# Two-layer graph network, 128 graphs: W3's product of the first quad by two levels of Winograd's form, a list of steps of its own for six periods, and another order within a period

## The chip, the cores and the metric

The kernel runs on one core of a Trainium2 chip. The metric is the device time of one launch in microseconds, lower is better. Everything is fp32.

## The reference

There are B = 128 graphs with N = 128 nodes and F = 512 features: x is [128, 128, 512], adj [128, 128, 128]. Two layers follow one another, each a residual step with a layer norm:

```python
deg = jnp.sum(adj, axis=-1, keepdims=True)                      # layer 0
agg = jnp.einsum('bij,bjf->bif', adj, x) / jnp.maximum(deg, 1e-6)
x = layernorm(x + relu(jnp.concatenate([x, agg], 2) @ W.T))     # W: 512 x 1024
h = relu(adj @ (x @ W1) + b1)                                   # layer 1
h = relu(adj @ (h @ W2) + b2)
x = layernorm(x + adj @ (h @ W3) + b3)                          # W1, W2, W3: 512 x 512
```

## The kernel before, in words

**Quads and products.** The graphs are taken in 32 quads of four (`NG = 32`, `G = 4`). Of a quad, the 512 x 512 matrix of its nodes and features is multiplied with each of the weights: twice for layer 0 (the halves of W that meet x and agg), then W1, W2, W3. Each is done in Winograd's form of Strassen's method. One level means seven products of blocks of 256, each of four matmuls 128x256 (`product`, L596), reached through `rows_a`/`rows_b` or `wino_a`/`wino_b`. Two levels mean that each of the seven is again split in seven, 49 matmuls in all, of 128x128 (`inner_product`, L614), reached through `single_a`/`single_b`. These need inner forms of both factors (`inner_sums`): those of the data are made for each quad by POOL, or by DVE, and lie in the small `ti` buffers; those of W2 and W3 are made once, on DVE, and lie in the large buffer `big` in place of the layer-0 weights `wb` and `wa`. From quad 2 on, the two layer-0 products are done together by two levels (`joint_a`/`joint_b`, matmuls 128x256 of L614), with forms of the weights that were written to DRAM once (`forms`) and stream back through the buffers `ring` and parts of `big`. Quads 0 and 1 do layer 0 by one level. In the kernel before, quad 0 does all of layer 1 by one level (`two(q)` is q >= 1), quads 1 to 30 do W2 and W3 by two levels and W1 by one, and quad 31 has forms of its own at the end.

**Stages.** The work of a quad is cut into stages, each a Python generator:

- X loads x transposed and makes its sums; D loads adj (`ar`), sums it to degrees on DVE (`deg`), sends their reciprocals to DRAM in another order (`dd<-deg`, elements of 4 bytes) and back to all partitions (`ah<-dd`); AT loads adj transposed (`at`).
- L0 to L3 are layer 0's products. A0 and A1 load x itself (`s<-in_x_dram`), copy the half of the product with x into a PSUM bank on ACT (L885), add adj times the other half on PE (L889), take relu and add x on DVE (L896), and do the layer norm (statistics on DVE, L828 and L829; the normalization on ACT, L859).
- G0 to G3 multiply with adj on PE (L914) and copy the result to SBUF; Ha and Hb are W1's product (L596); Sa and Sb W2's; H2 multiplies with adj (L1002) and applies bias and relu on ACT (L1013); Ta and Tb are W3's product; Z0 and Z1 multiply with adj (L1109), add the residual, do the second layer norm and store.

Between two groups of matmuls of a product the banks are moved: ACT copies a bank to SBUF (`copied`, L576) or to another bank that the next matmuls add to (`seeded`, L582), DVE adds a bank and a buffer (all of `add` for DVE has line L325, for POOL L327). All DMAs have line L318; SP issues nearly all of them, and waits in its queue for the buffer of each.

**The order of the work.** It is written before the kernel is emitted. `ORDER` is a list of stages with lags: "L3-4" in period t is the next part of stage L3 of quad t − 4. A period goes through the list once; a stage that comes up before its conditions hold (`AFTER`) is put off until they do. Steps create operations, and the class `Plan` then lists each engine's operations in a fixed order, by due times worked back from PE's and by costs that it assumes for each kind of operation. It has constants: `AHEAD` (how far down PE's list it may look), `HELP` (how late a POOL operation must be for DVE to take it), `REST`, and `LEADS` (how far ahead of their due time some operations may be listed); `SIZES` gives the numbers of buffers `s`, `v`, `ti` and `ring`. At run time each engine does its operations strictly in that order. `AFTER` says of W3's product only that it follows H2. Work that is done once hangs on finished stages (`posts`): layer 0's forms are made after L3 of quad 0, W2's inner forms after L2 and L3 of quad 1 and Sb of quad 0, W3's after L2 and L3 of quad 1 and Tb of quad 0.

Of the kernel before, what the change touches and what calls it, by code (L numbers as in the profile page):

```python
# [35 lines left out]
class Plan:  # L36
# [5 lines left out]


    LAG = 0.15
    AHEAD, HELP, HOLD, SEEN, REST, SPARE = 32, 16.0, 5.0, 8, 15.0, 1
    DMA_US, DMA_RATE = 2.0, 0.22e6

    def __init__(self, pools):
# [175 lines left out]


BANKS = 8
SIZES = 8, 3, 7, 6
LEADS = 6.9, 7.0, 29.0, 448.5
AFTER = {
    "X": "L2-1+1 L3-1+1", "D": "A0-1 A1-1 D-1", "AT": "Z0-2 Z1-2", "L0": "X D AT A1-1 A0-1 Z0-2 Z1-2", "L1": "L0", "L2": "L1", "L3": "L1 L2<2",  # L230
    "A0": "L2 L3", "A1": "L2 L3", "G0": "A0 Hb-1", "G1": "A0 Hb-1", "G2": "A1 Hb-1", "G3": "G0 G1 G2 A1",
    "Ha": "G3 Tb-1!", "Hb": "Ha", "Sa": "Hb Z0-1! Z1-1!", "Sb": "Sa", "H2": "Sb", "Ta": "H2", "Tb": "Ta", "Z0": "Ta Tb!", "Z1": "Tb",
}
ORDER = """
    L3-4 L0-4 Ta-6 H2-5 L3-4 Tb-5 Sa-5 L1-4 L1-4 Hb-5 D Tb-6 L2-4 L3-4 G0-4 Z0-6 Sb-4 D L2-4 L2-4 Tb-5 L0-3 L0-3 L1-4
    Ta-5 Ha-4 A1-4 L1-4 L3-3 Tb-5 Sb-4 X-3 Tb-5 A0-4 Ha-4 L2-4 L3-3 Ha-4 Ha-4 H2-5 H2-5 H2-5 Hb-4 L0-3 Tb-5 Tb-5 H2-5
    L3-4 L2-4 L2-4 Sb-4 L1-3 L2-4 L0-3 Z1-6 Sb-4 L3-3 Ta-5 Sb-4 Ta-5 G3-4 AT-3 A0-3 Ta-5 G2-4 Z0-5 L3-3 Z0-5 G2-4 Sa-4
    Ha-3 Ta-5 Tb-5 A1-4 Ha-3 Sb-4 G1-4 Sa-4 Sb-4 L0-3 G3-4 Sb-4 L1-3 Sa-4 Sa-4 Sa-4 Sa-4 Z1-5 A0-4 L1-3 G1-4 Z1-6 L2-3
    Hb-4 G0-4 AT-3 Ta-5 X-2 L1-3 Ta-5 L0-3 A1-3 Sa-4 L0-3
"""  # L240


# [1 line left out]
def gnn_resnorm_kernel(  # L244
# [16 lines left out]
    NG, F = x.shape[0], 512  # L261
# [7 lines left out]

    NS, NV, NI, NR = SIZES  # L270
    EARLY = 2
# [35 lines left out]
    def pinned(ins):  # L307
        return tc.keep_in_program_order(ins)
# [4 lines left out]
    def scalar(n, emit, reads, writes, columns=0, lead=None):  # L313
        plan.op("ACT", 0.165 + 0.00083 * n + 0.1 * columns, emit, reads, writes, lead=lead)

    def dma(dst, src, reads, writes, size, queue="SP", lead=None):
        eng = nc.sync if queue == "SP" else nc.scalar
        plan.op(queue, 0.06, lambda: pinned(eng.dma_start(dst(), src())), reads, writes, size=size, lead=lead)  # L318

    def const(v):  # L320
        return lambda: v

    def add(eng, n, dst, a, b, reads, writes, op=OP.add, shared=False, lead=None):

        on_vector = lambda: pinned(nc.vector.tensor_tensor(dst(), a(), b(), op=op))  # L325
        if eng == "POOL":
            on_gpsimd = lambda: pinned(nc.gpsimd.tensor_tensor(dst(), a(), b(), op=op))  # L327
            plan.op("POOL", 0.03 + 0.00243 * n, on_gpsimd, reads, writes, True, other=(0.06 + 0.00123 * n, on_vector), lead=lead)
        else:
            vector(n, on_vector, reads, writes, shared)  # L330
# [90 lines left out]
    class Streamed:  # L421

        def parts(self, ps, i):
# [3 lines left out]
                lambda: RING_T[s.index][:, 0:n], const(FORMS[i - 1][:, ps[0] : ps[-1] + 1].rearrange("p k s n -> p k (s n)")),  # L427
                ["ring free"] + [("form", w, i, p) for w in range(2) for p in ps], [s], n * P * H * 4, lead=LEADS[3],
            )
            return [lambda j=j: RING_T[s.index][:, j] for j in range(n)], [s]  # L430

    class Data:
# [18 lines left out]
        def inner_sums(self):  # L451
            for ps in PAIRS:
# [13 lines left out]
                for dst, a, b, reads, writes, op in (  # L466
# [4 lines left out]
                ):  # L471
                    add("POOL", n * P, dst, a, b, reads, writes, op, lead=LEADS[2] if dst is first else None)

# [38 lines left out]
    def data(q, name):  # L512
        if (q, name) not in TS:
            i = int(name != "g1")
            alone = q == NG - 1 and name != "g1"
            TS[q, name] = Data("xT", XT_T) if alone else Data(f"T{i}", T_T[i])
        return TS[q, name]

    def row(q, name):
        i = int(name != "y" and q < NG - 1)  # L520
        return Rows(f"row{i}", ROW_T[i])
# [46 lines left out]
    def quarters(p, n):  # L568
        return bank_ap(p).rearrange("p a (b n) -> p (a b) n", n=P)[:, 0:n]
# [50 lines left out]
    def v_part(v, n, g, c):  # L620
        return lambda: V_T[v.index][:, 0:n, g, c]
# [56 lines left out]
    def last_part(a, b, ps, joint, v, kv, sinks):  # L678
# [18 lines left out]

        scalar(n * P, lambda: pinned(nc.scalar.copy(quarters(pz, n), v_part(v, n, 1, 1)())), kv, [pz], lead=LEADS[0])
        add("POOL", n * P, v_part(v, n, 0, 1), v_part(v, n, 0, 1), v_part(v, n, 1, 1), kv, [(v, "d")], OP.subtract)
# [180 lines left out]
    def seg_agg(q, m):  # L880
        y, u = l0(q)
        for g in (2 * m, 2 * m + 1):
            p, r = Slot("bank", seeded=True), Slot("s", spare=3)
            dma(lambda r=r: S_T[r.index].rearrange("p a b -> p (a b)"), const(x[q][:, g]), (), [r], P * F * 4, lead=LEADS[1])
            scalar(512, lambda g=g, p=p: pinned(nc.scalar.copy(bank_ap(p), u.graph(g))), u.keys((g,)), [p], lead=LEADS[0])  # L885
            plan.op(
# [78 lines left out]
    def two(q):  # L965
        return q >= 1
# [25 lines left out]
    def seg_h2(q):  # L992
        d, s = data(q, "h2"), row(q, "s2")
        a, ka = at(q)
        for o in (2, 3, 0, 1):
            p = Slot("bank")
            h, c = o // 2, o % 2

            def emit(o=o, p=p):
                for g in range(G):  # L1000
                    r = pinned(
                        nc.tensor.matmul(  # L1002
                            bank_ap(p)[:, g // 2, (g % 2) * P : (g % 2 + 1) * P],
                            s.chunk(g, o), a[:, g, :], start=g == 0, stop=True, skip_group_check=True,
                        )
                    )
                return r

            plan.op("PE", 0.888, emit, ka + s.keys(cs=(o,)), [p])
            scalar(  # L1010
                512,
                lambda o=o, p=p, h=h, c=c: pinned(
                    nc.scalar.activation(  # L1013
                        d.t[:, 4 * h : 4 * h + 2, c], bank_ap(p).rearrange("p m (g n) -> p m g n", g=2), AF.Relu,
                        bias=B2_T[:, o : o + 1],
                    )
                ),
                [p, "b2"], d.keys((4 * h, 4 * h + 1), (c,)), columns=1,
            )
            yield  # L1020
        d.sums(at_end=q == NG - 1)
        if two(q) and q < NG - 1:
            d.inner_sums()

    def columns_a(key, a, b, t):
# [59 lines left out]
    def seg_s3_a(q):  # L1085
        if q == NG - 1:
            W3.restore()
            yield from rows_at_end_a(("s3", q), data(q, "h2"), W3, row(q, "s3"))
            return
        yield from (single_a if two(q) else rows_a)(("s3", q), data(q, "h2"), W3, row(q, "s3"))  # L1090

    def seg_s3_b(q):
        if q == NG - 1:
            yield from rows_at_end_b(("s3", q), data(q, "h2"), W3, row(q, "s3"))
            return
        yield from (single_b if two(q) else rows_b)(("s3", q), data(q, "h2"), W3, row(q, "s3"))

    def seg_last(q, m):
        s, u = row(q, "s3"), u_of(q)
# [2 lines left out]
        for j, o in enumerate(os):  # L1102
            g = 2 * m + j
            p = Slot("bank", seeded=True)
            scalar(512, lambda p=p: pinned(nc.scalar.copy(bank_ap(p).rearrange("p a b -> p (a b)"), B3_T)), ["b3"], [p], lead=LEADS[0])
            plan.op(
# [44 lines left out]
    W3 = Weight("w3", w3, ["row of degrees"])  # L1151
# [4 lines left out]
    GONE = [(w, p) for w in ("wb", "wa") for p in range(7)]  # L1156
# [25 lines left out]
    done = {(0, "X"), (0, "D"), (0, "AT")}  # L1182
# [10 lines left out]
    steps, late = {}, []  # L1193

    def ready(q, n):
        return all((q - lag, m) in done or not first <= q - lag < cap for m, lag, first, cap in after(n))

    def weights_to_forms():
# [3 lines left out]
    posts = [  # L1202
        ([(0, "L3")], weights_to_forms),
        ([(1, "L2"), (1, "L3"), (0, "Sb")], lambda: W2.inner_sums(GONE)),
        ([(1, "L2"), (1, "L3"), (0, "Tb")], lambda: W3.inner_sums(GONE + ["ring free"])),
    ]

    def step(q, n):
        if (q, n) not in steps:
            steps[q, n] = STAGES[n](q)  # L1210
        over = next(steps[q, n], "over") == "over"
        if over:
            done.add((q, n))
            for post in [p for p in posts if done.issuperset(p[0])]:
                posts.remove(post)
                post[1]()

    def catch_up():
        while True:
            i = next((i for i, w in enumerate(late) if w in done or ready(*w)), None)  # L1220
            if i is None:
                return
            w = late.pop(i)
            if w not in done:
                step(*w)

    tokens = [(w.partition("-")[0], int(w.partition("-")[2] or 0)) for w in ORDER.split()]
    for t in range(NG + max((lag for _, lag in tokens), default=0)):
        for n, lag in tokens:
            q = t - lag  # L1230
            if not 0 <= q < NG or (q, n) in done:
                continue
            if (q, n) in late or not ready(q, n):
                late.append((q, n))
            else:
                step(q, n)
                catch_up()
    while len(done) < NG * len(STAGES):
        step(*next((q, n) for q in range(NG) for n in sorted(STAGES) if (q, n) not in done and ready(q, n)))

# [47 lines left out]
```

## Time and profile before

| what | us |
|---|---|
| median of three runs | 2265.83 (2265.13 to 2266.15) |
| the profiled execution | 2261.35 |
| its span, first to last instruction | 2259.4 |
| PE busy | 2238.6 |
| DVE busy | 1632.7 |
| ACT busy | 1237.8 |
| POOL busy | 1112.0 |

The profile is of one execution. PE is TensorE, DVE VectorE, ACT ScalarE, POOL GpSimd, SP SyncE; "PEld" is the loading of weights into PE, beside its matmuls. A line such as L614 is a line of the kernel. In a timeline the columns are start, duration, engine, line, operation, output and inputs, shapes and count, and in brackets the idle time before with what ended it. Each matmul in fp32 leaves two records. The granted clock of PE was 0.999 of full speed in this execution. The kernel has three parts: a start up to about 133 us, in which the weights and the first quads come in; then a period that repeats each 69.6 us with the work of about one quad; and an end of a few us, in which the last quad's rows are normalized and stored.

### The profile page before, as it was taken

How to read it: one execution, taken by the hardware profiler on the slowest of the kernel's cores; microseconds unless marked ns; L12 is line 12 of the kernel's file. 1: busy time of each engine (PE TensorE's matmuls, PEld its weight loads, DVE VectorE, ACT ScalarE, POOL GpSimd, SP SyncE). 2: the span in 40 equal slices, each digit the busy share in tenths (PEclk: the TensorE clock that was granted, in tenths of full speed). 3: DMA queues.
4: the chain of work that ended last, by engine and by line, in shares of the span. 5: the costliest groups of instructions: out<-in, count | busy, mean ns of one | idle time of the engine just before them, and what ended most of it. 6: DMA issues, size and time to landing. Idle time of an engine off the chain costs nothing.

```text
span 2259.4 us, 39677 instructions
## 1 busy us (share of the span) xinstructions
PE 2238.6 (99%) x13620; PEld 1967.4 (87%) x13620; DVE 1632.7 (72%) x3552; ACT 1237.8 (55%) x2369; POOL 1112.0 (49%) x1400
## 2 busy tenths in 40 slices
PE   8999999999999999999999999999999999999998
PEld 7888888898898988988888889889898898888886
DVE  5677777777777777777777777777777777777675
ACT  2455555555555555555555555555555555555554
POOL 0245554545545455454555454654545545455540
PEclk9999999999999999999999999999999999999999
DMA  7744445534455444554444553445534455443431
GB/s 236 158 139 133 138 155 172 168 122 146 130 180 175 122 147 134 167 171 137 139 135 158 171 164 123 144 137 176 179 117 151 130 167 171 131 135 127 157 120 38
DMA packets 218615, 333.12 MB, mean 147 GB/s; under 512 B 39344, under 2 KB 84400, under 8 KB 218416
## 3 DMA queue, kind: packets, MB, share of 16 engines
q1 hardware_dynamic: 217744, 330.33, 47.5%
q8 instruction: 110, 1.80, 0.4%
q14 instruction: 89, 0.73, 0.2%
q10 hardware_dynamic: 672, 0.26, 0.1%
HBM read 290.46 MB, written 40.04 MB: 146 GB/s over the span
## 4 chain that ended last, share of the span: by engine, by line
PE 98%; DMA 1%; DVE 0%; issue 0%; ACT 0%; SPq 0%; ACTq 0%; DVEq 0%
PE bank L614 58%; PE bank L596 21%; PE bank L914 5%; PE bank L1002 5%; PE bank L1109 5%; PE bank L889 5%; DMA s<-in_x_dram 1%; DMA big<-in_w0T_dram 0%; DVE st L828 0%; DVE u L896 0%; DVE big L325 0%; SPq L318 0%; ACTq L1283 0%; ACT u L859 0%; ACT T L1013 0%
## 5 line engine op out<-in xcount | busy, mean ns | idle before, releaser
L576 ACT COPY s<-bank 128x384 f32<-128x384 f32 (+1 forms) x567 | 306.2, 540 | 428.7 <-PE bank L614 327.3
L596 PE MATMUL bank<-T,w 128*128 128x256 f32 x1792 | 411.7, 379 | 0.0
L596 PEld LDWEIGHTS bank<-T,w 128*128 128x128 f32 x1792 | 335.8, 190 | 68.9 <-issue 28.5
L327 POOL TENSOR_TENSOR xT<-xT 128x512 f32<-128x512 f32 (+1 forms) x244 | 236.6, 970 | 137.6 <-DVE ah L325 41.4
L325 DVE TENSOR_TENSOR v<-bank,s 128x512 f32<-128x512 f32 x240 | 162.7, 688 | 191.5 <-PE bank L614 133.9
L327 POOL TENSOR_TENSOR T<-T 128x512 f32<-128x512 f32 (+2 forms) x250 | 253.0, 1028 | 69.5 <-ACT T L925 38.1
L614 PE MATMUL bank<-big,ti 128*128 128x128 f32 (+1 forms) x1410 | 261.7, 317 | 0.0
L614 PE MATMUL bank<-big,xT 128*128 128x256 f32 x976 | 253.9, 380 | 1.1 <-DMA big<-forms 1.1
L582 ACT COPY bank<-bank 128x512 f32<-128x512 f32 (+2 forms) x273 | 142.9, 523 | 176.7 <-PE bank L614 124.4
L614 PEld LDWEIGHTS bank<-w,ti 128*128 128x128 f32 x1680 | 215.9, 192 | 18.9 <-issue 7.2
L614 PEld LDWEIGHTS bank<-big,T 128*128 128x128 f32 x1680 | 215.9, 191 | 15.5 <-issue 7.0
L327 POOL TENSOR_TENSOR v<-v 128x384 f32<-128x384 f32 (+2 forms) x90 | 88.9, 1002 | 284.0 <-DVE v L325 156.8
L614 PE MATMUL bank<-w,T 128*128 128x128 f32 x1680 | 228.2, 276 | 0.0
L614 PE MATMUL bank<-big,T 128*128 128x128 f32 x1680 | 223.9, 276 | 2.9
L614 PE MATMUL bank<-w,ti 128*128 128x128 f32 x1680 | 226.5, 275 | 0.0
L614 PEld LDWEIGHTS bank<-w,T 128*128 128x128 f32 x1680 | 213.6, 192 | 10.4 <-ACT bank L582 5.7
L614 PEld LDWEIGHTS bank<-big,ti 128*128 128x128 f32 x1410 | 204.6, 191 | 18.6 <-issue 4.8
L325 DVE TENSOR_TENSOR row<-bank,s 128x384 f32<-128x384 f32 (+2 forms) x254 | 118.8, 468 | 136.8 <-PE bank L614 91.8
L325 DVE TENSOR_TENSOR T<-T 128x512 f32<-128x512 f32 (+1 forms) x370 | 208.8, 585 | 4.9 <-ACT T L925 4.2
L327 POOL TENSOR_TENSOR s<-s,v 128x512 f32<-128x512 f32 (+1 forms) x60 | 68.1, 1135 | 282.1 <-DVE T L325 165.3
L614 PEld LDWEIGHTS bank<-big,xT 128*128 128x128 f32 x976 | 174.7, 190 | 19.6 <-DMA big<-forms 1.7
L325 DVE TENSOR_TENSOR v<-v 128x512 f32<-128x512 f32 (+1 forms) x270 | 179.1, 672 | 8.5 <-DVE v L325 0.5
(86 smaller groups left out, 4095.2 us busy)
## 6 DMA issues: line engine op xcount, KB each, us to landing
big<-forms SPq DMA_DIRECT2D x327, 256.0 KB, 3.7
ring<-forms SPq DMA_DIRECT2D x303, 256.0 KB, 3.7
s<-in_x_dram SPq DMA_DIRECT2D x128, 256.0 KB, 5.1
out_dram<-s SPq DMA_DIRECT2D x126, 256.0 KB, 3.5
xT<-in_xT_dram SPq DMA_DIRECT2D x62, 512.0 KB, 5.8
big<-forms SPq DMA_DIRECT2D x119, 128.0 KB, 2.2
ring<-forms SPq DMA_DIRECT2D x91, 128.0 KB, 2.7
ar<-in_adj_dram SPq DMA_DIRECT2D x32, 256.0 KB, 2.8
```

Of the source, the lines that this page charges most:

```text
L325: on_vector = lambda: pinned(nc.vector.tensor_tensor(dst(), a(), b(), op=op))
L327: on_gpsimd = lambda: pinned(nc.gpsimd.tensor_tensor(dst(), a(), b(), op=op))
L576: scalar(n * P, lambda: pinned(nc.scalar.copy(quarters_of(s, n), quarters(p, n))), [p], [s])
L582: scalar(n * P, lambda: pinned(nc.scalar.copy(quarters(s, n), quarters(p, n))), [p], [s])
L596: nc.tensor.matmul(bank_ap(p)[:, o, :], lhsT, rhs, start=start and o == 0 and c == 0, stop=c == 1, skip_group_check=True,)
L614: nc.tensor.matmul(dst, ta(), tb(), start=start and n == 0, stop=True, skip_group_check=True)
L889: nc.tensor.matmul(bank_ap(p), AH_T[:, g, :], y.graph(g), start=False, stop=True, skip_group_check=True)
L914: nc.tensor.matmul(bank_ap(p)[:, c // 2, (c % 2) * P : (c % 2 + 1) * P], u.chunk(g, c), a[:, g, :], start=c == 0, stop=True, skip_group_ch ...
L1002: nc.tensor.matmul(bank_ap(p)[:, g // 2, (g % 2) * P : (g % 2 + 1) * P], s.chunk(g, o), a[:, g, :], start=g == 0, stop=True, skip_group_ch ...
L1109: nc.tensor.matmul(bank_ap(p), a[:, g, :], s.graph(g), start=False, stop=True, skip_group_check=True)
```

## The change

Four things are changed.

1. W3's product of quad 0 is done by two levels, as that of the others: H2 of quad 0 makes inner forms (`seg_h2`), `seg_s3_a` and `seg_s3_b` use `single_a` and `single_b` for all quads but the last, W3's inner forms are made once L2 and L3 of quad 1 are done, and Ta of quad 0 waits for these two stages.
2. The first six periods are no longer taken from `ORDER`: `FIRST` lists the steps of the first six periods one by one, each as a stage and a quad ("Sb-1" is a part of Sb of quad 1). From period 6 on, `ORDER` is used.
3. `ORDER` is another list.
4. The planner's constants: `AHEAD` 32 to 20, `HELP` 16 to 12, `REST` 15 to 40; one more `s` buffer (8 to 9) and one fewer `ti` (7 to 6); other `LEADS`.

```diff
--- before.py
+++ after.py
@@ -42,7 +42,7 @@
 
 
     LAG = 0.15
-    AHEAD, HELP, HOLD, SEEN, REST, SPARE = 32, 16.0, 5.0, 8, 15.0, 1
+    AHEAD, HELP, HOLD, SEEN, REST, SPARE = 20, 12.0, 5.0, 8, 40.0, 1
     DMA_US, DMA_RATE = 2.0, 0.22e6
 
     def __init__(self, pools):
@@ -224,19 +224,30 @@
 
 
 BANKS = 8
-SIZES = 8, 3, 7, 6
-LEADS = 6.9, 7.0, 29.0, 448.5
+SIZES = 9, 3, 6, 6
+LEADS = 8.2, 7.0, 30.7, 456.0
 AFTER = {
     "X": "L2-1+1 L3-1+1", "D": "A0-1 A1-1 D-1", "AT": "Z0-2 Z1-2", "L0": "X D AT A1-1 A0-1 Z0-2 Z1-2", "L1": "L0", "L2": "L1", "L3": "L1 L2<2",
     "A0": "L2 L3", "A1": "L2 L3", "G0": "A0 Hb-1", "G1": "A0 Hb-1", "G2": "A1 Hb-1", "G3": "G0 G1 G2 A1",
-    "Ha": "G3 Tb-1!", "Hb": "Ha", "Sa": "Hb Z0-1! Z1-1!", "Sb": "Sa", "H2": "Sb", "Ta": "H2", "Tb": "Ta", "Z0": "Ta Tb!", "Z1": "Tb",
+    "Ha": "G3 Tb-1!", "Hb": "Ha", "Sa": "Hb Z0-1! Z1-1!", "Sb": "Sa", "H2": "Sb", "Ta": "H2 L2--1<2 L3--1<2", "Tb": "Ta", "Z0": "Ta Tb!", "Z1": "Tb",
 }
+FIRST, FROM = """
+    Sb-1 Sb-1 G2-0 L3-0 Ha-0 Ha-1 Ha-0 Ta-0 L3-0 L3-1 H2-0 L2-0 L1-0 Ha-0 L2-0 D-4 Ha-1 H2-0 Sb-1 L0-0 G0-1 D-2 Sb-0
+    Ha-0 G0-0 L2-0 L2-0 Ha-0 L1-0 Ta-0 Ta-0 L3-2 G1-1 L0-0 G0-0 Sa-0 G2-0 L0-0 Sa-0 Ha-0 Hb-1 L0-0 Tb-0 Sb-1 D-3 X-1
+    A1-0 L0-2 D-1 L0-2 Ta-0 L0-2 A0-0 H2-0 L1-0 Sa-1 D-4 Ha-1 L0-2 Ta-0 G3-1 L1-1 Sa-0 Sa-0 Ta-0 AT-1 X-3 L0-3 G1-0
+    L1-2 Sa-1 L0-0 G0-1 Z0-1 L0-2 G3-0 X-2 Sb-1 Sa-1 D-3 Z0-0 L3-0 L0-2 Sa-2 G1-0 H2-0 Sa-1 X-1 L3-2 X-3 G3-0 L1-1
+    L2-1 G0-2 Ta-0 Ha-1 D-1 Hb-0 L3-2 L2-1 L1-2 D-5 L0-2 Ha-1 Tb-0 Tb-0 L2-2 L3-1 L2-1 Tb-0 Ha-2 D-2 L0-0 L3-1 Sb-1
+    Sa-1 Sb-1 Sb-0 Sb-1 Z1-0 AT-2 L2-1 A1-1 Sa-0 A1-1 L2-1 D-5 L0-3 L0-1 L2-0 Ha-1 L0-1 Sa-0 G1-1 Z0-0 Hb-2 L0-1 L1-2
+    Ha-2 X-4 G0-3 L3-2 AT-2 Ha-2 Sb-2 L1-1 Sb-2 L0-1 L0-2 A0-0 Sb-0 G2-1 Z0-0 L2-1 L0-1 L0-3 AT-1 Sa-1 A1-0 Sa-1 A1-0
+    L0-3 Tb-0 G2-1 L0-1 A0-1 Sa-2 A0-1 L0-3 Sb-2 L3-3 Sb-2 H2-0 G0-2 A1-1 G3-1 A0-0 Hb-1 L3-2 L2-2 Tb-0 G2-2 G1-2 Z0-2
+    Hb-3 L2-2 Hb-0 Sb-2 L1-3 A0-1 L2-0 X-2 Hb-0 Sb-2 L1-2 Tb-1 A1-2 Sa-1 Sa-2 H2-1 Sb-3 Tb-0 Sb-3 Sb-3
+""", 6
 ORDER = """
-    L3-4 L0-4 Ta-6 H2-5 L3-4 Tb-5 Sa-5 L1-4 L1-4 Hb-5 D Tb-6 L2-4 L3-4 G0-4 Z0-6 Sb-4 D L2-4 L2-4 Tb-5 L0-3 L0-3 L1-4
-    Ta-5 Ha-4 A1-4 L1-4 L3-3 Tb-5 Sb-4 X-3 Tb-5 A0-4 Ha-4 L2-4 L3-3 Ha-4 Ha-4 H2-5 H2-5 H2-5 Hb-4 L0-3 Tb-5 Tb-5 H2-5
-    L3-4 L2-4 L2-4 Sb-4 L1-3 L2-4 L0-3 Z1-6 Sb-4 L3-3 Ta-5 Sb-4 Ta-5 G3-4 AT-3 A0-3 Ta-5 G2-4 Z0-5 L3-3 Z0-5 G2-4 Sa-4
-    Ha-3 Ta-5 Tb-5 A1-4 Ha-3 Sb-4 G1-4 Sa-4 Sb-4 L0-3 G3-4 Sb-4 L1-3 Sa-4 Sa-4 Sa-4 Sa-4 Z1-5 A0-4 L1-3 G1-4 Z1-6 L2-3
-    Hb-4 G0-4 AT-3 Ta-5 X-2 L1-3 Ta-5 L0-3 A1-3 Sa-4 L0-3
+    L1-4 L3-3 D Sa-4 G2-3 L2-4 L0-3 Ta-6 L2-4 Hb-5 L2-4 Ha-4 L0-3 Tb-6 Ta-5 L1-4 L3-2 L1-4 Tb-5 L3-4 Ha-4 L1-4 G3-4
+    L2-3 L1-3 Z0-5 D Sa-3 Sb-3 Z1-6 Tb-5 Z1-5 G3-4 Sa-4 H2-5 L0-2 Tb-5 Sb-3 L3-4 H2-5 Sa-3 H2-5 H2-5 AT-3 L2-4 L1-3
+    Hb-4 Tb-5 Tb-5 L3-3 L3-4 G2-4 G1-4 L0-3 G0-3 L0-2 Z0-3 Sb-4 Ha-4 L2-4 L3-3 X-2 A1-4 Ta-5 A0-4 Ta-5 A0-4 Sa-4 Hb-2
+    Ta-5 A1-4 A0-4 Ha-3 L0-2 G1-3 AT-3 Sb-2 Ta-5 Z1-6 H2-4 X-1 Sb-3 Ta-5 Tb-5 Ha-3 L3-3 Sa-4 G0-2 L2-3 Sb-2 L1-3 Sb-4
+    Sa-4 Sb-2 Ha-3 Sa-3 L0-2 Ta-5 A1-3 L2-3 Z0-5 Tb-4 L1-2 L0-2
 """
 
 
@@ -1019,7 +1030,7 @@
             )
             yield
         d.sums(at_end=q == NG - 1)
-        if two(q) and q < NG - 1:
+        if q < NG - 1:
             d.inner_sums()
 
     def columns_a(key, a, b, t):
@@ -1087,13 +1098,13 @@
             W3.restore()
             yield from rows_at_end_a(("s3", q), data(q, "h2"), W3, row(q, "s3"))
             return
-        yield from (single_a if two(q) else rows_a)(("s3", q), data(q, "h2"), W3, row(q, "s3"))
+        yield from (single_a)(("s3", q), data(q, "h2"), W3, row(q, "s3"))
 
     def seg_s3_b(q):
         if q == NG - 1:
             yield from rows_at_end_b(("s3", q), data(q, "h2"), W3, row(q, "s3"))
             return
-        yield from (single_b if two(q) else rows_b)(("s3", q), data(q, "h2"), W3, row(q, "s3"))
+        yield from (single_b)(("s3", q), data(q, "h2"), W3, row(q, "s3"))
 
     def seg_last(q, m):
         s, u = row(q, "s3"), u_of(q)
@@ -1202,7 +1213,7 @@
     posts = [
         ([(0, "L3")], weights_to_forms),
         ([(1, "L2"), (1, "L3"), (0, "Sb")], lambda: W2.inner_sums(GONE)),
-        ([(1, "L2"), (1, "L3"), (0, "Tb")], lambda: W3.inner_sums(GONE + ["ring free"])),
+        ([(1, "L2"), (1, "L3")], lambda: W3.inner_sums(GONE + ["ring free"])),
     ]
 
     def step(q, n):
@@ -1225,16 +1236,16 @@
                 step(*w)
 
     tokens = [(w.partition("-")[0], int(w.partition("-")[2] or 0)) for w in ORDER.split()]
-    for t in range(NG + max((lag for _, lag in tokens), default=0)):
-        for n, lag in tokens:
-            q = t - lag
-            if not 0 <= q < NG or (q, n) in done:
-                continue
-            if (q, n) in late or not ready(q, n):
-                late.append((q, n))
-            else:
-                step(q, n)
-                catch_up()
+    first = [(w.partition("-")[0], int(w.partition("-")[2])) for w in FIRST.split()]
+    periods = range(FROM, NG + max((lag for _, lag in tokens), default=0))
+    for n, q in first + [(n, t - lag) for t in periods for n, lag in tokens]:
+        if not 0 <= q < NG or (q, n) in done:
+            continue
+        if (q, n) in late or not ready(q, n):
+            late.append((q, n))
+        else:
+            step(q, n)
+            catch_up()
     while len(done) < NG * len(STAGES):
         step(*next((q, n) for q in range(NG) for n in sorted(STAGES) if (q, n) not in done and ready(q, n)))
 
```

W1's and W2's products of quad 0 stay at one level. Counted in the built programs, PE has 6831 matmuls in place of 6810: 49 more of 128x128 in L614's place, 28 fewer of 128x256 in L596's. DVE has 2577 additions of two tensors in place of 2555, POOL 1399 in place of 1396, ACT 1602 copies in place of 1598; SP issues 1369 DMAs in both.

## The prediction

> **What bounds the kernel now.** I read the page first, then the chain of waits.
>
> ```profile
> PE 2238.6 (99%) x13620; PEld 1967.4 (87%) x13620; DVE 1632.7 (72%) x3552; ACT 1237.8 (55%) x2369; POOL 1112.0 (49%) x1400
> PE 98%; DMA 1%; DVE 0%; issue 0%; ACT 0%; SPq 0%; ACTq 0%; DVEq 0%
> ```
>
> PE is busy 99% and is 98% of the chain, so only two things can shorten the run: less PE work, or smaller gaps between PE's instructions. Chain of waits in one period (start, duration, what):
>
> ```profile
> 203.10 21.75 PE bank L614 x148
> ...
> 238.94 3.43 PE bank L889 x8
> ...
> 244.83 0.10 issue
> ...
> 248.96 1.79 PE bank L914 x16
> ...
> 254.96 1.73 PE bank L596 x8
> ...
> 272.68 0.22 PE bank L614
> ```
>
> A matmul in fp32 leaves two records. By these rows a record is .112 us at width 128 (1.79/16), .216 at 256 (1.73/8) and .429 at 512 (3.43/8). A period starts each 69.58 us (272.68 − 203.10). It holds 260 records of width 128 (196 of L614, 32 of L914, 32 of L1002), 154 of 256 (98 of L614, 56 of L596) and 16 of 512: 260×.1118 + 154×.2158 + 16×.429 = 69.17 us. So **.42 us of a period is gaps**. They stay invisible in PE's busy time, since a matmul's recorded end is late; start to start shows them (PE's timeline, then ACT's):
>
> ```profile
> 236.05 1.08 PE L614 MATMUL bank<-ring,xT 128*128 128x256 f32 x4
> 236.96 1.11 PE L614 MATMUL bank<-w,T 128*128 128x128 f32 x8
> 237.91 1.03 PE L614 MATMUL bank<-big,ti 128*128 128x256 f32 x4
> ...
> 243.99 0.83 PE L614 MATMUL bank<-w,T 128*128 128x128 f32 x6
> 244.92 1.13 PE L614 MATMUL bank<-big,T 128*128 128x128 f32 x8
> ```
>
> ```profile
> 244.19 0.58 ACT L576 COPY s<-bank 128x512 f32<-128x512 f32 x1 [3.65 <-PE bank L614]
> ```
>
> Six records (.67 us) begin at 243.99, yet the next group begins .93 later: the copy L576 of the bank filled before 243.99 runs 244.19 to 244.77, and PE needs that bank. The edge costs .20 (PE to ACT) + .58 + .15 (ACT to PE) = .93, with .67 of PE work to cover it: .26 lost. The next group loses .07 the same way (copy of 384), and 236.05 and 236.96 lose .05 each (.91 for .86, .95 for .895): .43 in all.
>
> Before period 1 (133.5) I compared PE's starts with the sum of its work: apart from the first loads and a cold start, one pause of 3.64 us, in 104.9 to 112.3 (4.29 of 7.40 us busy). Its waits, and what SP and DVE did (timelines):
>
> ```profile
> PE bank L914 <- ACT u L859: 2.0, 1, 2.0
> PE bank L614 <- DMA big<-forms: 1.1, 1, 1.1
> ```
>
> ```profile
> 90.79 0.37 SPq L318 DMA_DIRECT2D dd<-deg  x1
> 91.25 1.89 SPq L318 DMA_DIRECT2D s<-in_x_dram  x4
> ```
>
> ```profile
> 102.32 0.69 DVE L896 SCALAR_TENSOR_TENSOR u<-bank,s 128x512 f32<-128x512 f32 x1 [5.41 <-DMA s<-in_x_dram]
> ```
>
> The x of quad 1 is issued right behind a store of degrees and lands 11 us later, where x takes 5.1 in the median; DVE, LN (L859) and L914 are late in turn.
>
> **What the Trainium skill says.** "TensorE: Matmul & The Clock Gate", Architectural detail: PE's queue can pull weight loads ahead of matmuls, ScalarE and VectorE are strict FIFO. The trace agrees: 1967 us of loads vanish under PE. So ACT's place in line counts, not only its load of 55%. "Perfetto Trace Analysis", Tensor Engine Instruction: PE's ends are estimated; here a group of .67 reads .83. "DMA: Bandwidth & Descriptors", Specifications: below 512 B a write is read-modify-write; and Queues, rings and completion order: a ring is consumed in order and a semaphore lands after all earlier writes of its engine. The trace fits: dd<-deg is 512 elements of 4 bytes, 10.0 us to landing, and loads behind it take 11 to 13.
>
> **The change, part by part.**
>
> *W3's product of quad 0.* One level is 28 matmuls of 256 (2×.2158 = .4316): 12.085 us. Two levels are 49 of 128 (.2236): 10.956. **−1.13 us**, all on PE's path. Added beside it: inner forms of h2 for quad 0 (POOL .46 to 1.0 us each, partly moved to DVE at .69 or less) and copies on ACT (.585). The changed order has their last result half a microsecond or more ahead of PE's need; before period 1 POOL is nearly idle (17 of 90 us in 15 to 104.9), so zero. W3's inner forms, 8 DVE operations (about 4.8 us), move some 30 us earlier; DVE is busy 51 of 90 there: zero, or at most 1 if they hold a sum back.
>
> *The new period.* PE work is the same 69.17. I went through the changed order of every engine for PE → copy → PE edges and compared the PE work between with the price: .94 for a copy of 512 (.2 + .585 + .15), .82 for 384 (.463). Tightest now: .89 and .86, both with copies of 384, so no gap; all other ACT edges have 1.33 or more. The gaps go: 30 periods × .42 = **−12.7 us**. New: L1109 follows a DVE sum of 384 (.557) with .86 between; price .2 + .557 + .15 = .91, so .05 a period, 30 × .045 = **+1.3** (0 to 3: the bracket .15 to .20 for a wake-up). Longer chains (A → LN → G → H1 → W2 → W3, inner forms on POOL) show .3 us or more of slack each; SIZES gives one more `s` buffer and one fewer `ti`, within that slack. Streamed forms: the shortest time from a buffer's release by PE to its use is 3.45 us, twice in a row with 128 KB, against 3.52 before without a gap; landing takes 2.2 to 2.7 plus issue .33 and wake-up: zero. Degrees: in steady periods no load follows dd<-deg for some 15 us, before and after alike.
>
> *The start.* For the new list I put times on SP's queue from the PE work ahead plus the 9.95 us that before shows there. x of quad 1 (4 loads) now stands behind dd of quad 2, issued at 73 to 76, landing by 85 to 92 even at 11 to 15.6 us; its LN feeds L914 near 94.7, whose x must be there by about 91 to 92.6. **−3.64**, margin 1 to 4. But dd of quads 3 and 4 are now issued back to back near 118, both behind a big<-forms load on SP. Queued behind them: a ring<-forms load (released 120.8) that PE needs at 130.9, and adj of a later quad, for which DVE's reduce waits, ahead of a DVE sum needed at 136. If the two slow spells overlap (11 us), the load lands at 131: 0 to 1.5 us. If they add (20), at 138: 5 to 9. No row shows two in a row. I take **+3.5**, range 0 to 9.
>
> Sum: −1.13 − 12.7 + 1.3 − 3.64 + 3.5 = **−12.7**. The profiled execution was 2261.35 (span 2259.4), so 2248.7; the median lies 4.48 above that execution, and I assume the same: 2265.83 − 12.7 = **2253.2**.
>
> **Rivals.**
> 1. *No pause at the start* (each load overtakes dd): 2253.2 − 3.5 = 2249.7; without the DVE edge 2248.4. For: DMA moves only 39 GB/s around 90. Against: x at 91.25.
> 2. *The two dd in full*: +9, DVE edge 3: 2253.2 + 5.5 + 1.7 = 2260.4.
> 3. *The gap moves instead of going*: another edge of .35 to .45 takes its place (a copy queued behind another on ACT, whose order is fixed): 2253.2 + 30 × .38 = 2264.6, or, if the start is worse too, 2267. Against: ACT 39 of 70 us a period.
> 4. *Slower: the pair of streamed forms with 3.45 us lands late.* PE would wait at one place of every period. Before, 3.52 sufficed for a single load; a landing of 4.0 in place of 2.7 (256 KB shows 3.7 to 4.1), with .33 issue and .2 + .15 wake-up, is 4.7, or 1.2 late. All that only undoes the gain up to 12.7/30 = .42 a period; it is measurably slower from .42 + 4.5/30 = .57. At .7: 2274.
> 5. *Nothing changes* (the steady order works out equal): 2264.6 as in 3; the diff's new list and period do reach the engine orders, so this is part of 3.
>
> **How the numbers follow.** Main case .47 (2253.2), rival 1 .19, rival 2 .17, rival 3 .09, rival 4 .08. A measurement of this kernel tells about 0.2%, 4.5 us: faster means under 2261.3. The main case, rival 1 and nearly all of rival 2 lie there: .82; rival 3 and the top of 2: .10; slower .08. The range 2247 to 2261.5 holds the first three cases: no edge and no pause with 1.4 us to spare at the bottom, rival 2 at the top; about 0.17 lies outside above.
>
> **What would show it.** Right: the chain's period is 69.2 in place of 69.58; no group of six L614 records followed by a .93 start; by the old line numbers L614 has 5978 records of width 128 and L596 2184 in all (98 more, 56 fewer); PE <- ACT u L859 is gone from the early waits and x of quad 1 lands by 92. Between 118 and 140 SP's timeline shows two dd<-deg, and PE's waits at most one ring<-forms. Wrong: a period over 69.4, with its wait in PE's starts ahead of L1109 or of a big<-forms or ring<-forms group; or waits for DMA of over 5 us before 140.

## The result, and the profile after

The changed kernel takes 2259.74 us (median of 8 runs, 2257.91 to 2261.28) beside 2265.99 for the kernel before (8 runs, 2261.82 to 2267.45): ratio 0.9972, 95% interval 0.9963 to 0.9981, 6.25 us less. The forecast was 2253.2, 12.6 less. It went the way that was forecast and lies in the range, but only half of the gain came. Each later comparison was made on one chip, with the kernel before beside it; the kernel before took 2260.1 to 2266 in them, so only differences from the before of the same comparison are used.

The page of the profiled execution (2260.83 us, span 2259.1; line numbers are 11 higher than before from L576 on):

```profile
PE 2236.4 (99%) x13662; PEld 1966.2 (87%) x13662; DVE 1617.9 (72%) x3574; ACT 1240.4 (55%) x2373; POOL 1077.8 (48%) x1403
PE 98%; DMA 1%; DVE 0%; ACT 0%; issue 0%; SPq 0%; ACTq 0%; DVEq 0%
```

PE is the bound as before, and 42 records more (98 − 56) are there as counted. Waits of PE (us in all, times, longest):

```profile
PE bank L625 <- DMA ring<-forms: 6.5, 2, 6.2
...
PE bank L607 <- ACT bank L593: 0.7, 1, 0.7
PE bank L625 <- DMA big<-forms: 0.4, 1, 0.4
```

The waits for the late x (L914 on ACT, L614 on big<-forms) are gone. A new one of 6.2 us stands in their place. SP's and PE's timelines show where:

```profile
119.16 0.32 SPq L329 DMA_DIRECT2D big<-forms  x1
119.57 0.94 SPq L329 DMA_DIRECT2D dd<-deg  x2
122.56 0.33 SPq L329 DMA_DIRECT2D ring<-forms  x1
```

```profile
131.77 1.05 PE L625 MATMUL bank<-w,T 128*128 128x128 f32 x8
139.07 3.75 PE L625 MATMUL bank<-ring,xT 128*128 128x256 f32 x8 [6.25 <-DMA ring<-forms]
142.61 1.68 PE L625 MATMUL bank<-w,T 128*128 128x128 f32 x8
```

There are two stores of degrees in a row, then the load of forms; PE gets it 16.5 us after its issue. And the eight records after the pause begin 3.54 us ahead of the next group (142.61) in place of 1.73. The windows show why: PEclk, after the five engines' columns, is .50 there (behind it stand the busy share of the DMA engines and what they moved, in GB/s).

```profile
130.00:139.00 9.00, 2.82 (x17) 2.38 (x15) 5.37 (x11) 0.85 (x3) 3.51 (x6) 0.89 0.33 26
139.00:143.00 4.00, 3.93 (x10) 3.24 (x11) 3.60 (x11) 2.21 (x7) 0.05 (x1) 0.50 0.76 256
```

The periods of the chain of waits (start, duration):

```profile
345.92 23.65 PE bank L625 x156
...
415.67 23.53 PE bank L625 x156
...
485.00 23.53 PE bank L625 x156
...
554.34 23.53 PE bank L625 x156
```

A period takes 69.33 or 69.34 us from the second line on; the one before it took 69.75, and some others are longer too. So the period fell by .24 where .38 was forecast.

What the two profiled executions differ by, from PE's starts (the time from each record's start to the next, less what a record of its width takes):

| term | forecast | measured |
|---|---|---|
| PE work | −1.1 | −1.1 |
| gaps of 30 periods | −11.4 | −7.3 |
| streamed forms that land late, four periods | 0 | +1.8 |
| old pause of the start | −3.6 | −3.6 |
| pause near 132, with the slow clock behind it | +3.5 | +8.8 |
| smaller new waits at the start | 0 | +1.2 |
| sum | −12.7 | −0.2 |
| executions, 2261.35 to 2260.83 | | −0.5 |

The profiled executions are almost equal, while the medians differ by 6.25.

### The profile page after: what moved, and what is told of

It is laid out like the page before. It is cut to its first block, busy times and chain, and to the rows that moved or that the text cites. A ratio compares the mean times of both kernels' runs of the same rounds, so it can differ in the third digit from the quotient of the medians.

```text
span 2259.1 us, 40108 instructions
## 1 busy us (share of the span) xinstructions
PE 2236.4 (99%) x13662; PEld 1966.2 (87%) x13662; DVE 1617.9 (72%) x3574; ACT 1240.4 (55%) x2373; POOL 1077.8 (48%) x1403
## 4 chain that ended last, share of the span: by engine, by line
PE 98%; DMA 1%; DVE 0%; ACT 0%; issue 0%; SPq 0%; ACTq 0%; DVEq 0%
PE bank L625 58%; PE bank L607 21%; PE bank L925 5%; PE bank L1013 5%; PE bank L1120 5%; PE bank L900 5%; DMA ring<-forms 1%; DMA big<-in_w0T_dram 0%; DMA big<-forms 0%; DVE big L336 0%; SPq L329 0%; DVE st L839 0%; DVE T L336 0%; DVE s L336 0%; ACT s L860 0%
## 5 line engine op out<-in xcount | busy, mean ns | idle before, releaser
L587 ACT COPY s<-bank 128x512 f32<-128x512 f32 (+1 forms) x568 | 307.2, 541 | 383.0 <-PE bank L625 264.8
L607 PE MATMUL bank<-T,w 128*128 128x256 f32 x1792 | 408.1, 379 | 0.7 <-ACT bank L593 0.7
L607 PEld LDWEIGHTS bank<-T,w 128*128 128x128 f32 x1792 | 333.2, 190 | 55.5 <-issue 14.6
L338 POOL TENSOR_TENSOR xT<-xT 128x512 f32<-128x512 f32 (+1 forms) x244 | 247.4, 1020 | 76.2 <-DVE rstd L851 36.8
L625 PEld LDWEIGHTS bank<-w,T 128*128 128x128 f32 x1708 | 222.7, 192 | 20.8 <-issue 14.1
L336 DVE TENSOR_TENSOR T<-T 128x512 f32<-128x512 f32 (+2 forms) x408 | 234.0, 598 | 8.0 <-ACT T L936 6.2
L338 POOL TENSOR_TENSOR T<-T 128x512 f32<-128x512 f32 (+2 forms) x216 | 197.3, 934 | 77.7 <-DVE T L336 40.1
L625 PE MATMUL bank<-ring,xT 128*128 128x256 f32 x848 | 218.1, 382 | 6.2 <-DMA ring<-forms 6.2
L625 PE MATMUL bank<-big,xT 128*128 128x256 f32 x832 | 220.7, 380 | 0.5 <-DMA big<-forms 0.4
L336 DVE TENSOR_TENSOR v<-v 128x512 f32<-128x512 f32 x303 | 192.6, 643 | 1.1
L625 PE MATMUL bank<-ring,ti 128*128 128x256 f32 x732 | 188.9, 379 | 0.3 <-DMA ring<-forms 0.3
L338 POOL TENSOR_TENSOR v<-v 128x384 f32<-128x384 f32 (+1 forms) x61 | 69.3, 1136 | 247.2 <-DVE u L336 129.1
```

The costliest lines, as they stand in the source:

```text
L587: scalar(n * P, lambda: pinned(nc.scalar.copy(quarters_of(s, n), quarters(p, n))), [p], [s])
L607: nc.tensor.matmul(bank_ap(p)[:, o, :], lhsT, rhs, start=start and o == 0 and c == 0, stop=c == 1, skip_group_check=True,)
L625: nc.tensor.matmul(dst, ta(), tb(), start=start and n == 0, stop=True, skip_group_check=True)
```

## The experiments

**The first four** ask what the pause at 132 is, and what the usual execution of before looks like. In all that move an operation, the list that the planner made is changed in place just before it is emitted, by a helper `move(o, after)`; every other operation keeps its order. `DEG[q]` holds the operations of quad q's degrees (sum, maximum, reciprocal, `dd<-deg`, `ah<-dd`), `AR[q]` the load of its adj; the lines that fill them are not shown.

*before_again*: no edit.

> The kernel before, unchanged, profiled once more: its profiled execution was 2261.35 us, 4.6 under the median of its runs, so its profile does not show what most executions spend. If the difference is at the start (loads behind dd<-deg landing later than in the first profile), the pause before L914 near 105 to 112 us is 6 to 9 us here in place of 3.64 and the steady period stays at 69.58 us. If it is spread, by streamed forms that land late now and then, the period averages 69.7 and the start stays at 3.6.

Measured: 2260.34 us, beside 2260.14 (median of 25 runs); pause at the start 2.9 us, period 69.58. Neither theory holds: here the median of before is that of its profile. In the first set of runs before was slower; nothing in the traces says by what.

*dd_early*:

```diff
-    for o in plan.order():
+    ops = plan.order()
...
+    for q, place in ((3, DEG[2][4]), (4, AR[5])):
+        red, top, rec, out, _ = DEG[q]
+        move(top, red)
+        move(rec, top)
+        move(out, place)
+
+    for o in ops:
```

> The changed kernel with six tiny DVE operations and two DMAs moved, nothing else: maximum and reciprocal of the degrees of quads 3 and 4 stand right behind their sums on DVE, and their dd<-deg are issued some 25 and 5 us earlier, each by itself and ahead of the loads that PE needs next. Theory (the two dd<-deg in a row hold the ring<-forms load behind them for 16 us): the wait of 6.4 us near 132 us goes, and with it 2.4 us of slow clock after it; the profiled execution falls from 2260.83 to about 2252, the median from 2259.7 to about 2251.5. Rival (that load is late by itself, for its buffer or for the other loads around it): the wait stays, within 1 us, and so does the time.

Measured: 2250.87 us (2250.37 to 2251.28), ratio to before 0.9957 (0.9944 to 0.9969). SP's timeline now:

```profile
112.20 0.33 SPq L329 DMA_DIRECT2D ar<-in_adj_dram  x1
113.11 0.37 SPq L329 DMA_DIRECT2D dd<-deg  x1
119.05 0.32 SPq L329 DMA_DIRECT2D big<-forms  x1
122.45 0.32 SPq L329 DMA_DIRECT2D ring<-forms  x1
```

The same load is issued at the same time, and PE has no wait for it: it goes on with the ring group at 132.56. With two DMAs of 2 KB elsewhere the kernel is 9.3 us under before, where the changed kernel was 6.25. The maximum and reciprocal on DVE moved too, but dd_act (below) moves the same ones and keeps the pause: the pause is the two stores'.

*before_dd_early*: the kernel before, with its list changed alike:

```diff
+    red, top, rec, out, _ = DEG[3]
+    on_vector = [o for o in ops if o.engine == "DVE"]
+    move(red, on_vector[on_vector.index(red) - 4])
+    move(top, red)
+    move(rec, top)
+    move(out, rec)
```

> The kernel before with one thing moved: the sum, maximum and reciprocal of quad 3's degrees some 8 us earlier on DVE, so that its dd<-deg is issued near 80 us in place of 90.8, ahead of the x loads of quad 1 by as much. Theory (x is held by that store): the pause of 3.64 us at 104.9 to 112.3 goes; the profiled execution is about 2258, the median 2262 or, if the 4.6 us by which the median of before lies above its profile also come from this pause, 2258. Rival (big<-forms is as late without it): 1 to 2 us remain, 2264.

Measured: 2257.51 us (21 runs), ratio 0.9989 (0.9982 to 0.9995), 2.6 less. dd<-deg goes at 80.53 and the first x at 83.98, PE's waits at 105 to 112 are gone: the pause came from the late x, at the size that before_again shows (2.9). What made x late is not parted by this run: the store still stands just ahead of x on SP, and a load of x still takes 9.2 us to landing (11 before), but x is issued up to 7.3 us earlier. In the kernel before SP had also waited 2.5 us for the reciprocals before it could issue the store and then x.

*after_one_level*: the changed kernel, with `single_a if two(q) else rows_a` (and `_b`), `if two(q) and q < NG - 1`, the old AFTER of Ta and the old condition for W3's inner forms put back.

> The changed kernel with W3's product of quad 0 by one level as before, all else of the change kept (new list, order, constants): PE has 1.13 us more work. Counted by work alone it is 1.1 us slower than the changed kernel, 2260.9. But the operations of the start fall into other places, and if the pause near 132 us is a matter of where the two dd<-deg fall and not of the product, it may be gone: then about 2252.5.

Measured: 2252.04 us, ratio 0.9962 (0.9950 to 0.9975). The pause is gone: SP issues one dd<-deg at 89.59, the next at 104.89. It is 8.1 us under before, the changed kernel 6.25 (3.75 in after_again, below): W3's product by two levels, which saves 1.13 us of matmuls, made the whole slower by where the planner then put two stores. Against dd_early, where neither has the pause, two levels gain 1.2 us (2252.04 − 2250.87, on one chip; the runs of the two overlap by .1 us), about the work counted.

**The next four** ask whether the first comparison's 6.25 us holds, how two stores hold a load, and what the first part of the change does alone.

*after_again*: no edit.

> The changed kernel unchanged, timed once more beside the kernel before. The first comparison gave -6.25 us (2265.99 to 2259.74), while the two profiled executions differ by 0.5 (2261.35 to 2260.83). If the profiles are typical and the first comparison's before had time in it that comes from where it ran, the difference here is 0 to 1 us (before 2260.1, this 2259.5). If 6 us are the rule, this is 2254 where before is 2260.

Measured: 2256.31 us (20 runs, 2253.99 to 2258.66) beside 2260.06: ratio 0.9983 (0.9976 to 0.9990), 3.75 less. This lies between the two expectations. The profiled execution took 2257.98 and shows the pause in another form:

```profile
PE bank L625 <- DVE st L839: 3.0, 1, 3.0
PE bank L625 <- ACT s L587: 1.0, 1, 1.0
```

DVE stood for 7.8 us on a sum of degrees that may not overwrite what dd<-deg still reads, and everything behind it on DVE was late (its timeline):

```profile
131.57 0.69 DVE L563 TENSOR_REDUCE deg<-ar 128x4 f32<-128x512 f32 x1 [7.80 <-DMA dd<-deg]
```

So the stores reach PE by two ways, the load and the sum, and which comes last varies. The runs of this kernel spread over 4.7 us here, those of before over 2.8; in the first comparison it was 3.4 and 5.6, so the spread by itself shows nothing.

*dd_act*, dd<-deg of quads 3 and 4 on ACT's queue (maximum and reciprocal moved up as in dd_early):

```diff
-        plan.op(queue, 0.06, lambda: pinned(eng.dma_start(dst(), src())), reads, writes, size=size, lead=lead)
+        return plan.op(queue, 0.06, lambda: pinned((nc.scalar if ring else eng).dma_start(dst(), src())), reads, writes, size=size, lead=lead)
...
-        dma(const(dd.rearrange("g i -> i g")), const(d), kd, [("dd", q % 2)], 400000 if q else 1600000, queue)
+        out = dma(const(dd.rearrange("g i -> i g")), const(d), kd, [("dd", q % 2)], 400000 if q else 1600000, queue, ring=q in (3, 4))
```

> The changed kernel with dd<-deg of quads 3 and 4 issued by ACT's queue in place of SP's, one behind the other at about the old place (their maximum and reciprocal made earlier on DVE so that ACT doesn't wait). If the loads are held by the order of SP's ring, they no longer stand behind the two stores: the wait of 6.4 us near 132 goes, about 2251. If the 16 DMA engines themselves are held by these stores, whichever ring they come from, the ring<-forms load is late all the same: a wait of 4 to 7 us near 132 stays, 2257 to 2260.

Measured: 2257.15 us (one run). ACT issues the stores at 117.99 and 119.86, SP the load at 121.32 from a ring with no store in it, and PE waits (timeline):

```profile
130.54 1.05 PE L628 MATMUL bank<-w,T 128*128 128x128 f32 x8
136.41 3.47 PE L628 MATMUL bank<-ring,xT 128*128 128x256 f32 x8 [4.82 <-DMA ring<-forms]
```

It took 15.1 us from issue to use, against 16.5. The data itself creeps: here are four microseconds of this run, then the same of dd_early, with no store just ahead of the load (the last number is GB/s).

```profile
122.00:126.00 4.00, 4.00 (x15) 2.58 (x15) 0.56 (x1) 2.59 (x6) 4.00 (x6) 1.00 0.27 48
```

```profile
122.00:126.00 4.00, 4.00 (x19) 2.89 (x19) 2.13 (x5) 2.90 (x7) 3.92 (x7) 1.00 0.53 128
```

In the next two stretches of 4 us dd_act has 32 and 26. It is not the order of a ring; transfers of another queue are held as well, though what in the DMA engines holds them isn't shown. The Trainium skill has the shared engines ("DMA: Bandwidth & Descriptors", Issuing engines are not separate DMA queues: DMAs of all issuing engines run on the same 16 engines), and this run agrees.

*dd_one*: dd_early without quad 4, whose store stays ahead of the load.

> The changed kernel with quad 3's dd<-deg alone issued earlier (near 91 us); quad 4's stays directly ahead of the ring<-forms load, near 119.5. If the two spells add, one alone ends at about 130, and the load lands in time or up to 1.5 us late: 2251 to 2253. If one store is enough to hold the load for its 16 us, the wait stays at 6 us: 2260.

Measured: 2249.63 us (one run; before 2260.06). The store goes at 118.37, the load at 121.19, PE uses it 10.1 us later, at 131.29, and hasn't waited. One store is hidden; two add up. That it is 1.2 us below dd_early says nothing of the second store: by PE's starts the first 60 us lost 3.8 us in this execution and 5.1 in dd_early's, before any of the moved stores.

*before_two_levels*: the kernel before, with only the first part of the change (`seg_h2`, `seg_s3_a`, `seg_s3_b`, AFTER of Ta, the condition of W3's inner forms).

> The kernel before with one part of the change alone: W3's product of quad 0 by two levels, its inner forms once quad 1's layer 0 is done; list, order and constants as before. By work alone it would be 1.1 us faster than before. Rival: the planner assigns buffers and due times from what it has listed so far, and with the old list the later periods come out in another order with gaps of some 3 us in each: 2330 or more.

Measured: 2320.7 us (one run), with some 2.3 us of gaps in a period; PE's longest sum of waits in it:

```profile
PE bank L614 <- DVE T L325: 25.6, 29, 0.9
```

The rival was right, its size somewhat lower. With the old list and constants the product of one quad could not be changed alone; with the new ones it does no such harm (dd_early).

**The last four** ask what a gap of the period costs, and whether the parts add up.

*before_moved*, one group of four matmuls moved two places down PE's list in each of 30 periods (the other engines keep their orders):

```diff
+    MOVED = [(410, 30, 2)]
...
+    for first, times, by in MOVED:
+        for k in range(times):
+            o = before_it[first + 215 * k]
+            i = on_pe.index(o)
+            on_pe.insert(i + by, on_pe.pop(i))
```

`before_it[n]` is the group that starts at PE's matmul n; a period has 215 matmuls.

> The kernel before with one group moved in each of 30 periods: four matmuls of 128x128 (.89 us) go from ahead of a pair of groups to between them, so that 1.56 us of PE work cover the copy L576 in place of .67. Theory (the largest gap of the old period is the price of that copy: .25 from PE to ACT, .585 copy, .225 until PE goes on with its weights loaded, together 1.06, against .67): the gap of .26 and the .07 behind it go in every period, the period falls from 69.58 to 69.25, the time by 30 x .33 = 9.9 us, 2260 to 2250. Rival (PE runs into another wait at once, for a transfer or the next copy): at most a third of that, 2257.

Measured: 2251.86 us beside 2261.81, ratio 0.9958 (0.9945 to 0.9970), 9.95 less. Period 69.25 (chain: 202.86 to 272.11). PE's timeline at the place shown for before, then ACT's:

```profile
242.86 0.83 PE L614 MATMUL bank<-w,T 128*128 128x128 f32 x6
243.53 1.06 PE L614 MATMUL bank<-w,ti 128*128 128x128 f32 x8
244.43 1.06 PE L614 MATMUL bank<-big,T 128*128 128x128 f32 x8
245.32 0.83 PE L614 MATMUL bank<-big,ti 128*128 128x128 f32 x6
```

```profile
243.06 0.59 ACT L576 COPY s<-bank 128x512 f32<-128x512 f32 x1 [2.76 <-PE bank L614]
```

From 242.86 to 243.53 it is .67, and each group of eight takes .89 or .90: the .93 is gone, and so is the .07 that the group behind it lost. That .07 was not a second copy, as the prediction had it: in the trace of before it lies on the first record of the group, .185 in place of .112, so it is the rest of the same wait, paid when PE starts again. One edge of the old period (from PE to a copy and back to PE) was worth more than the whole change.

*before_both*: before_moved and before_dd_early in one.

> The kernel before with that group moved and with quad 3's degrees earlier at the start as in before_dd_early. If the two are separate, their gains add: -9.9 and -2.6 of before, 2260 to 2247.6, less than the changed kernel with its start mended (2250.9). If mending the start only lets the next transfer be late, 2250.

Measured: 2249.25 us, ratio 0.9943 (0.9929 to 0.9956), 12.56 less; expected 12.5. They add.

*best*: dd_one, and `MOVED = [(775, 28, 4)]` in the loop of before_moved.

> The changed kernel with quad 3's dd<-deg earlier (as dd_one, 2249.63 in one run) and one pair of matmuls (L625, 128x256, .86 us) moved behind the four groups that follow it in 28 periods, so that the group that follows a copy of 384 has more PE work ahead of it. Theory: that edge (.25 + .463 + .225 = .94 against .86) costs .068 a period; 28 x .068 = 1.9 us less than dd_one, 2247.7. Rival (the .068 is no wait but a property of the group): 2249.6. The .127 a period at L1120 stays in both.

Measured: 2248.85 us beside 2261.81, ratio 0.9941 (0.9929 to 0.9954), 12.96 less, where dd_one in its single run was 10.4 under its before. In PE's starts the excess of most periods over their work falls from .197 to .128: the .068 is gone. Median and dd_one's one run, on two chips, can't show 1.9 us apart; the starts do. It has the lowest median of this study, but before_both, the kernel before with two moves, is only .4 behind and the runs of the two overlap.

*after_no_first*:

```diff
-FIRST, FROM = """ ... """, 6
+FIRST, FROM = "", 0
```

> The changed kernel without its list for the first six periods: its ORDER is used from period 0. The steady period is that of the changed kernel, 69.33 us, if it doesn't hang on how it was entered. The start has its own pauses: if the two dd<-deg stand back to back here too, 5 to 9 us of pause before 150 us, 2256 to 2262; if not, 2252.

Measured: 2257.3 us (one run; before 2261.81). The gaps of a period are the same as the changed kernel's (.195). The start loses some 6 us, but not by two dd<-deg in a row; each stands alone, at 91.31 and 126.03:

```profile
PE bank L615 <- POOL T L328: 1.9, 1, 1.9
```

Inner forms are late there, and PE runs slow after this wait, with two smaller waits to come (PEclk .65 in 99 to 103 and .50 in 103 to 107). The expectation gave the time of its first case for a reason that isn't there: a miss. FIRST avoids this pause; with W3's product by two levels it has the one near 132 in its place.

## Why the prediction was wrong, and what in it was right

**Right.** PE is the bound and its work is as counted: records, −1.13 us (dd_early against after_one_level gives 1.17). The old period lost .42 us in gaps, and most of it at one copy: before_moved gets .33 back by one move. The late x of quad 1 was the old pause, and with the new list it is early. The danger at 118 to 139 was named with its DMAs, its load and DVE's sum behind them; a wait for DMA of over 5 us before 140 was among its signs of being wrong, and came.

**Step "I take +3.5, range 0 to 9".** In the profiled execution this is the largest mis-sized term: it measured 8.8, 5.3 too much. Two spells add (dd_one against the changed kernel), so the load lands at 139.0, as the bad case had it (138). The wait is 6.4 in PE's starts; the other 2.4 us are the clock of PE, halved for the first 4.8 us of work after the pause (to 143.9), which no step counted. The skill states it ("TensorE: Matmul & The Clock Gate", Part 1: half clock after an idle window of about 3.4 us, full clock after a busy one); the 6.25 us of idle and PEclk .50 agree. (In after_no_first a wait of 1.9 us, shorter than that figure, halved it too; there the measurement decides.) The working knew that the two stores were issued together, but no trace of before had two in a row; it took a value below the middle of its range, where the runs show that two add.

In medians the term is smaller: dd_early and dd_one against the changed kernel, each from its before, give 3.0 to 6.7 for pause and clock together. So the pause is only part of the miss. Without it the prediction's own sum is −16.2; dd_early and dd_one, which don't have it, are 9.3 and 10.4 under before. The missing 6 to 7 us are the next steps.

The prediction also put the hold down to the order of the ring. dd_act shows that another ring doesn't help.

**Step "price .94 for a copy of 512, .82 for 384" and "so .05 a period".** This is the second mis-sized term: −7.3 in place of −11.4. The price was too low at both ends. In the trace of before the copy L576 ends at 244.77, and PE, due at 244.66, loses .33 in two steps: it goes on at full pace .22 after the copy's end, not .15, as if its weights were loaded only then. In after, the copy of 384 starts at 223.11, .25 behind PE's next group. With .25 + .463 + .225 = .94 that edge of .86, taken as free, costs .068 a period. (The other edge, of .89, shows no loss, though by this price it should; the price isn't exact.) At L1109 (L1120 after), .26 + .557 + .165 = .98 against .86 costs .127 where .045 was taken. .20 in place of .05 by these two is 4.5 us in 30 periods; it explains −7.3 in place of −11.4. The same price, 1.06 for a copy of 512, is what foretold before_moved, and best takes the .068 away. That weight loads are the cause is read from the trace, not tried by itself.

**Steps taken at zero.** "Streamed forms: zero": in the profiled execution four periods wait for a load, .2 to .6 us each, 1.8 us in all (before_again none). This is rival 4 in small: it comes in some periods, not in each, and far from .57. The start has smaller new waits of 1.2 us, the longest for a copy (the .7 at L607 above), which the sum doesn't have either.

Rival 2, both stores in full and a dearer edge at L1109, was given .17. Its +9 for the pause and 3 for that edge are close to the measured 8.8 and 3.8 (30 × .127). Its 2260.4 is close to the median too, but by luck: the last step, on the median, failed as well.

**Step "the median lies 4.48 above that execution, and I assume the same".** This failed the other way. In its profile the changed kernel gains 0.5; in medians 6.25 and 3.75. Before's first profiled execution lay below all its runs of the first set; the second (before_again) lies at its median; the changed kernel's lay 1.1 and 1.7 above its medians, perhaps since its pause varies. Why before took 2266 in the first set is open. So it is in part luck that half of the forecast gain was measured: the errors of the terms add up to 12.4 us in the profiled execution, and the median of before, slow in that set, hides half of it.

## What to carry to other kernels

When an order is written by a planner, a part that saves work can cost several times its worth by moving two small transfers; look at what stands directly ahead of each load that the critical engine waits for, and count small stores ahead of it one by one. Price an edge between engines by what the trace shows from start to start at such an edge, the restart with it, and look for one group to move before rewriting the list: here one group gave 10 us. And before predicting a fraction of a per cent from one execution, ask where in the spread of runs it lies.

## What the runs showed of the hardware

- A store of 512 elements of 4 bytes, which itself takes about 10 us to landing (9.7 from ACT's queue in dd_act), holds other transfers for about as long, whichever queue issues it: a load of 256 KB that takes 4.0 us in the median took 15.1 behind two such stores of another queue, 16.5 behind two of its own; behind one it was there within 10.1.
- A pause of 6.2 us halved PE's clock for the first 4.8 us of work after it (2.4 us lost). Shorter ones did it too: waits of 3.0 and 1.0 close together (after_again), and one of 1.9 (after_no_first, where PEclk is .50 at 100.2, before the next wait). The waits of 1.1 and 2.0 of the old start left it at 1.00. What decides between these is open.
- After a wait, PE's first record takes .07 to .10 longer than its width does (.185 for .112 at 244.92 of before); the price of an edge is larger than the sum of its two hand-overs by that.
